# A fused attention and recurrence kernel: the last 128 queries turned token-major, batch statistics merged from three groups, and the recurrence's chunks started 10 steps ahead instead of 12

## The chip, the cores and the metric

The kernel runs on one core of one Trainium2 chip. The metric is the device time of one execution in microseconds. Each core has TensorE (PE, matrix products), VectorE (DVE), ScalarE (ACT), GpSimd (POOL) and SyncE (SP), which here only issues transfers. Each engine works through its own queue in order and waits for the others by semaphores; an instruction that waits holds up everything behind it on its engine.

## The reference, cut to what matters

```python
x = x + attention0(group_norm(x))            # 4 images, 128 channels, 64*64 pixels, full softmax
t = tokens(x)                                # (4, 4096, 128)
t = t + causal_attention(layer_norm(t))
l = layer_norm(t)
Wx = l @ W.T                                 # (4, 4096, 128)
mean, var = Wx.reshape(-1, 128).mean(0), Wx.reshape(-1, 128).var(0)   # over all 16384 tokens
Wx = (Wx - mean) * rsqrt(var + 1e-5) * gamma + beta
y = 0                                        # (4, 128)
for k in range(4096):
    y = sigmoid(Wx[:, k] + y @ V.T)          # V is orthogonal
    ys[:, k] = y
out = t + ys
```

Two things tie the end of the kernel together: the batch statistics need every token's `Wx`, that of the last token too, and the loop over 4096 tokens is serial in each of the four batches.

## The kernel before, in words

**Layout.** Data stand channel-major: 128 channels on the partitions, tokens along the free dimension. Attention goes batch by batch (`b`), layer by layer, in tiles of 512 queries (`c`), and inside a tile in units (`u`) of two key blocks of 128. `score(i)` makes the unit's scores on TensorE (`ps`) and their exponentials on ScalarE (`s`, with the causal mask of a diagonal block put on by GpSimd). `product(i)` adds `s` into the running `total` on VectorE and multiplies by the values on TensorE (`av`). The loop runs `score(i)`, a `step()` of side work, `product(i - 1)`. There are three buffers of `s`, so that an exponential waits for the add three units before it.

**The last tile.** The last 512 queries of the last batch are split into 384 and 128 (`LAST = 384`). The end of a tile is `finish` (divide by the sum of exponentials), `project` (W1v and the residual: `X2`), and `ffn` (deviation of each token, `FWc`, and the product of both into `WX`). For the last 128 queries before the change: the sums of exponentials are made for all 128 partitions by a product of `ones` with `total` (`pz`), inverted by a 128x128 reciprocal, multiplied with `av`, projected, transposed back to tokens for the deviation (`pt_f`), and the deviation is spread over the partitions by a product (`prow`). Then `bn_stats` goes over the last 512 columns, and `bn_aggr` over all 32 chunks' statistics (`fstats`), and from these come `fgain` and `fbias` of the batch normalization. `rsqrt` is one VectorE add and one GpSimd power.

**The recurrence.** Each batch's 4096 tokens are cut into chunks of 16, 16, 32 and 32 (`CHUNK`), and all chunks of a batch advance together. A chunk's start state is not known, so each starts from 0.5 and runs `WARM` steps on the tokens before its own; a sigmoid's slope is at most 1/4 and V keeps lengths, so that what is wrong at the start shrinks by four or more a step. At the end the states reached by the warm-up (`first`, `firstp`) are compared with the true ones (`ok`, bound `SAME = 2.0e-6`); if any differs by more, a general kernel is run after it. There are three chains side by side: batch 0, batch 1, and batches 2 and 3 together. One step of a chain is a product with V into PSUM (two passes, on top of the normalized input that VectorE has put there: `seed`) and one sigmoid on ScalarE (`move`, L1095). After `WARM` + 16 steps of all three, batches 2 and 3 go on alone for 16 more. `residual` adds the states to the kept activations and `store` sends them out.

`idle` issues products with zeros, whose results are not used. The tile framework orders the instructions of each engine and sets the semaphores; in a stretch under `manual_schedule` the order is that of the code.

## Time and profile before

| what | value |
|---|---|
| median of 3 runs | 2515.57 us (2515.12 to 2515.63) |
| profiled execution, its own time | 2515.47 us |
| its span, first to last instruction | 2513.7 us |
| mean granted TensorE clock | 0.997 |
| PE, DVE, ACT, POOL busy | 98%, 72%, 45%, 8% of the span |
| last product with values starts | 2432.45 us |
| first sigmoid of the recurrence starts | 2443.73 us |
| first sigmoid that writes a chunk's own token | 2459.20 us |
| batches 2 and 3 alone, from | about 2481 us |
| last residual ends, stores issued | 2498.96 us |

The profiled execution took 1.77 us more than its span, and lies 0.10 us under the median. In the profile's rows a line such as L995 is a line of the kernel's file; `out<-in` are the program's tile names without numbers; a fp32 product stands as two rows, one for each pass. The timeline view lists instructions in order of their start, merged where the same one repeats; its first two columns are start and duration in microseconds.

### The profile page before, as it was taken

What the parts mean: (1) busy time and instruction counts of PE and PEld (TensorE: products, weight loads), DVE (VectorE), ACT (ScalarE), POOL (GpSimd) and SP (SyncE); (2) the same over time, 40 slices, a digit from 0 to 9 for tenths busy, and PEclk for the clock granted to TensorE, in tenths of its full rate; (3) what the DMA queues carried; (4) which work ended last, traced back from release to release, by engine and by line L of the source; (5) the groups of instructions that cost most, each with busy time, mean ns of one, the idle gap of its engine ahead of it and who ended that gap; (6) DMA issues with size and microseconds to landing.
All of it is one profiled execution on the core that took longest, in us unless ns stands there. A gap on an engine that the chain in (4) does not pass through costs nothing.

```text
span 2513.7 us, 22498 instructions
## 1 busy us (share of the span) xinstructions
PE 2474.0 (98%) x7360; PEld 1342.9 (53%) x7360; DVE 1797.7 (72%) x3597; ACT 1121.9 (45%) x1399; POOL 210.8 (8%) x281
## 2 busy tenths in 40 slices
PE   7999999999999999999999999999999999999997
PEld 4555554444555555444455555444455555544465
DVE  6776669765877667866687676876677676786667
ACT  4444444444444444444444444444444444443456
POOL 2010002110000100210000010121000000010000
PEclk9999999999999999999999999999999999999998
DMA  2000001000100000100110000101010000010023
GB/s 75 9 17 9 17 9 42 21 22 13 46 17 9 17 9 22 36 24 13 35 33 14 12 13 13 34 25 26 13 46 17 9 17 9 17 26 17 9 76 136
DMA packets 154078, 64.40 MB, mean 26 GB/s; under 512 B 136160, under 2 KB 136928, under 8 KB 152160
## 3 DMA queue, kind: packets, MB, share of 16 engines
q1 hardware_dynamic: 151344, 59.27, 8.8%
q10 hardware_dynamic: 2608, 3.61, 0.4%
q8 instruction: 60, 0.98, 0.2%
q14 instruction: 66, 0.54, 0.1%
HBM read 31.66 MB, written 31.20 MB: 25 GB/s over the span
## 4 chain that ended last, share of the span: by engine, by line
PE 92%; DVE 4%; ACT 2%; issue 1%; POOL 1%; DMA 0%; SPq 0%; DVEq 0%; POOLq 0%
PE av L995 51%; PE ps L957 19%; PE ps L950 17%; PE pw_f L802 1%; PE pv L675 1%; PE pk L659 1%; PE pq L762 1%; PE po L858 1%; DVE total L992 1%; ACT WX L1095 1%; PE pz L1094 0%; ACT first L1095 0%; POOL X L656 0%; ACT WXp L1095 0%; DMA X<-in_x 0%
## 5 line engine op out<-in xcount | busy, mean ns | idle before, releaser
L992 DVE TENSOR_TENSOR total<-total,s 128x1024 f32<-128x1024 f32 (+5 forms) x810 | 882.9, 1094 | 537.7 <-ACT s L959 308.0
L995 PE MATMUL av<-s,WXp 128*128 128x512 f32 x2048 | 961.9, 592 | 0.0
L959 ACT ACTIVATE s<-ps,shift 128x1024 f32<-128x1024 f32 x512 | 569.9, 1114 | 759.5 <-PE ps L957 741.0
L957 PE MATMUL ps<-q,K 128*128 128x512 f32 x2048 | 757.9, 492 | 1.7 <-DVE K L670 1.6
L963 ACT ACTIVATE s<-ps,zero,R 128x512 f32<-128x512 f32 (+3 forms) x607 | 405.5, 718 | 510.6 <-PE ps L950 508.5
L995 PEld LDWEIGHTS av<-s,WXp 128*128 128x128 f32 x2048 | 384.2, 188 | 301.7 <-issue 259.9
L957 PEld LDWEIGHTS ps<-q,K 128*128 128x128 f32 x2048 | 386.0, 189 | 290.7 <-issue 232.3
L995 PE MATMUL av<-s,V 128*128 128x512 f32 (+3 forms) x1214 | 504.8, 538 | 1.3 <-POOL s L966 0.7
L950 PE MATMUL ps<-q,X 128*128 128x512 f32 (+3 forms) x1214 | 503.5, 537 | 0.0
L950 PEld LDWEIGHTS ps<-q,X 128*128 128x128 f32 x1214 | 224.9, 190 | 236.3 <-issue 219.5
L995 PEld LDWEIGHTS av<-s,V 128*128 128x128 f32 x1214 | 223.6, 190 | 230.5 <-issue 205.7
L571 POOL TENSOR_TENSOR rstd<-rstd,mhalf 128x4 f32<-128x4 f32 x32 | 32.4, 1012 | 1049.3 <-DVE rstd L570 1049.3
L966 POOL TENSOR_SCALAR_AFFINE_SELECT s<-s 128x128 f32<-128x128 f32 x128 | 52.5, 417 | 456.4 <-ACT s L963 455.8
L571 POOL TENSOR_TENSOR rstd_f<-rstd_f,mhalf 128x4 f32<-128x4 f32 (+2 forms) x33 | 47.4, 1436 | 507.9 <-DVE rstd_f L570 487.3
L656 POOL TENSOR_SCALAR X<-X,B0v 128x512 f32<-128x512 f32 x32 | 65.8, 2060 | 99.9 <-DVE xg L654 98.4
L754 DVE TENSOR_SCALAR V<-V,lmv,rstd 128x128 f32<-128x128 f32 x128 | 38.0, 342 | 33.6 <-POOL rstd L571 33.5
L689 DVE TENSOR_TENSOR q<-QR,qh 64x512 fp32r<-64x512 f32 x64 | 43.9, 686 | 6.7 <-PE ps L957 5.6
L671 ACT CAST K<-kh 64x512 fp32r<-64x512 f32 x32 | 19.7, 617 | 64.8 <-DVE kh L669 64.7
L826 DVE TENSOR_TENSOR t<-total 128x512 f32<-128x512 f32 x64 | 44.1, 689 | 4.4 <-PE pfw L615 2.5
L828 DVE STREAM_TRANSPOSE tt<-t 128x512 f32<-128x512 f32 x64 | 45.1, 705 | 1.6
L841 DVE STREAM_TRANSPOSE rb<-z 128x512 f32<-128x512 f32 x64 | 44.9, 702 | 1.0
L843 DVE SCALAR_TENSOR_TENSOR o<-rb,av 128x512 f32<-128x512 f32 x64 | 43.5, 680 | 2.7 <-DVE rb L841 0.5
(157 smaller groups left out, 1267.3 us busy)
## 6 DMA issues: line engine op xcount, KB each, us to landing
turn<-t SPq DMA_DIRECT2D x32, 256.0 KB, 2.0
V<-turn SPq DMA_DIRECT2D x128, 64.0 KB, 2.4
turn_f<-t_f SPq DMA_DIRECT2D x31, 256.0 KB, 2.0
t_f<-turn_f SPq DMA_DIRECT2D x124, 64.0 KB, 2.5
X<-in_x SPq DMA_DIRECT2D x28, 256.0 KB, 5.2
kept<-X SPq DMA_DIRECT2D x24, 256.0 KB, 2.0
Y<-kept SPq DMA_DIRECT2D x6, 1024.0 KB, 7.0
out<-Y SPq DMA_DIRECT2D x5, 1024.0 KB, 6.1
```

Of the source, the lines that this page charges most:

```text
L571: nc.gpsimd.tensor_tensor(dst, dst, mhalf[:, :n], ALU.pow)
L656: nc.gpsimd.tensor_scalar(xt, xt, B0v, None, ALU.add)
L826: nc.vector.tensor_tensor(t, total[:, 0, :w], total[:, 1, :w], ALU.add)
L828: nc.vector.transpose(tt, t)
L841: nc.vector.transpose(rb, z[:, :k].unsqueeze(2).to_broadcast([P, k, 32]))
L950: nc.tensor.matmul(ps[:, h, first[h] : w], lhsT=lhsT, rhs=q[:, off + first[h] : off + w], start=True, stop=True,)
L957: nc.tensor.matmul(ps[:, h, :], lhsT=lhsT, rhs=q[:, k, :], start=k == 0, stop=k == 1)
L959: nc.scalar.activation(s, ps, AF.Exp, bias=shift)
L963: nc.scalar.activation(part, ps[:, h, first[h] : w], AF.Exp, scale=scale, bias=zero)
L966: nc.gpsimd.affine_select(out=edge, in_=edge, pattern=[[1, P]], base=0, channel_multiplier=-1, compare_op=ALU.is_ge, fill=0.0,)
L992: nc.vector.tensor_tensor(t, t, s[:, h, f:w], ALU.add)
L995: nc.tensor.matmul(av[:, first[h] : w], lhsT=V[:, 2 * u + h, :], rhs=s[:, h, first[h] : w], start=u == 0 and h == 0, stop=2 * u + h == n - 1,)
```

## The change

The change touches only what surrounds the last 128 queries and the start of the recurrence.

1. `WARM` is 10 instead of 12.
2. The first step of every chunk needs no product: the state before it is 0.5 everywhere, so that V times it is a constant, added to beta once (`Fb0`, made in `merge1`). `first_step` is one ScalarE sigmoid from `WX` with the gain as scale. For all chunks but the last three of batch 3 it uses a gain and bias from the statistics without the last 128 queries (`scales["guess"]`); for those three it waits for the final ones.
3. The statistics have three groups in one tile `groups`: all full chunks but the last (`most_stats`, one `bn_aggr`), the 384 queries, and the 128 queries. `scale(9, ...)` gives the guess and `scale(15, ...)` the final gain.
4. The last 128 queries end in `last_part`, in an order written by hand. The sum of exponentials is a column with one token a partition (`pz_last`, products with one column of `ones`), the projection is made twice, once with tokens on the partitions (for the deviation) and once with channels (for `X2`), and the old activations are transposed ahead (`last_tokens`).
5. The states live in one tile `states` (768 columns, in the place of `QR`), cleared by GpSimd early. `pz_last` takes the last unit's exponentials directly, so the last add into `total` is gone.

```diff
-WARM = 12
+WARM = 10
...
+    def first_step(b, at, n, scales):
+        gain, bias = scales
+        l = CHUNK[b] - WARM
+        src = WX[b][:, l // 2, ds(at, n), l % 2]
+        nc.scalar.activation(first[b][:, ds(at + 1, n)], src, AF.Sigmoid, scale=gain, bias=bias)
...
+            nc.vector.bn_stats(groups[:, 3:9], WX[b][:, :, ds(c * QT // CHUNK[b], LAST // CHUNK[b]), :])
+            yield
+            whole(("most",))
+            gain, less = scale(9, "guess")
+            scales["guess"] = gain, shifted(gain, less, Fb0, "guess")
...
+        def scale(n, name):
+            mv = small.tile([P, 2], F32, name=f"mv_{name}")
+            nc.vector.bn_aggr(mv, groups[:, :n])
+            gain = const.tile([P, 1], F32, name=f"gain_{name}")
+            rsqrt(gain, mv[:, 1:2], 1e-5, 1)
+            less = const.tile([P, 1], F32, name=f"less_{name}")
+            nc.vector.tensor_scalar(less, mv[:, 0:1], -1.0, None, ALU.mult)
+            nc.vector.tensor_tensor(gain, gain, Fgamma, ALU.mult)
+            return gain, less
+
+        def most_stats():
...
+            nc.vector.bn_aggr(mv, stats_f.rearrange("p c s -> p (c s)"))
+            nc.vector.tensor_copy(groups[:, 1:2], mv[:, 0:1])
+            nc.vector.tensor_scalar(groups[:, 2:3], mv[:, 1:2], float(B * N - QT), None, ALU.mult)
...
+        def last_tokens():
+            pt = misc("pt_last")
+            nc.tensor.transpose(pt[:, :P], X[B - 1][:, ds(N - P, P)], ident)
+            scales["tok"] = tok = small.tile([P, C], F32, name="tok_last")
+            nc.scalar.copy(tok, pt[:, :P])
...
+        def last_part(av, pz, s):
...
+            avs = tmp.tile([P, QT], F32, tag="a", name="avs")[:, :w]
+            nc.vector.tensor_copy(avs, av[:, :w])
+            nc.scalar.activation(small.tile([P, 1], F32, name="sig"), s[:, 1, w - 1 : w], AF.Sigmoid)
+            for b in range(2):
+                first_step(b, 0, NC[b] - 1, scales["guess"])
+            rz = small.tile([P, 1], F32, name="rz")
+            nc.vector.reciprocal(rz, pz[:, 0:1])
+            ptok = wide[0][:, 0, :w]
+            nc.tensor.matmul(ptok, lhsT=avs, rhs=W1v, start=True, stop=True)
+            prz = wide[1][:, 0, :w]
+            nc.tensor.matmul(prz, lhsT=rz.to_broadcast([P, P]), rhs=ident, start=True, stop=True)
+            po = misc("po_last")[:, :w]
+            nc.tensor.matmul(po, lhsT=W1v, rhs=avs, start=True, stop=True)
+            idle(misc("idle_last"), 3)
+            tok = scales["tok"]
+            nc.vector.scalar_tensor_tensor(tok, ptok, rz, tok, ALU.mult, ALU.add)
+            rzs = tmp.tile([P, QT], F32, tag="b", name="rzs")[:, :w]
+            nc.scalar.copy(rzs, prz)
+            for b in range(2, B):
+                first_step(b, 0, NC[b] - 1 - (BEHIND if b == B - 1 else 0), scales["guess"])
...
+            nc.vector.bn_stats(stats, tok)
+            nc.vector.bn_aggr(mv, stats)
+            rsqrt(rstd, mv[:, 1:2], 1e-5, 1)
+            nc.vector.scalar_tensor_tensor(rzs, rzs, GUARD, po, ALU.mult, ALU.mult)
+            nc.vector.scalar_tensor_tensor(x2, rzs, 1.0 / GUARD, xt, ALU.mult, ALU.add)
+            nc.tensor.matmul(pw, lhsT=FWc, rhs=x2, start=True, stop=True)
+            prow = wide[0][:, 1, :w]
+            nc.tensor.matmul(prow, lhsT=rstd.to_broadcast([P, P]), rhs=ident, start=True, stop=True)
+            idle(misc("idle_last2"), 2)
+            nc.scalar.copy(raw, pw)
...
+            nc.vector.bn_stats(groups[:, 9:15], part)
+            scales["all"] = scale(15, "all")
...
-            if w == QT - LAST:
-                pz = misc(f"pz_{name}")
-                for h in range(2):
-                    nc.tensor.matmul(pz[:, :w], lhsT=ones, rhs=total[:, h, :w], start=h == 0, stop=h == 1)
-                idle(misc(f"idle_{name}"), 4)
-                rb = tmp.tile([P, QT], F32, tag="a", name=f"rb_{name}")[:, :w]
-                nc.vector.reciprocal(rb, pz[:, :w])
...
+            if last:
+                pz = misc("pz_last")
+                for h in range(2):
+                    nc.tensor.matmul(pz[:, 0:1], lhsT=total[:, h, :w], rhs=ones[:, 0:1], start=h == 0, stop=False)
...
+            if last:
+                for h in range(2):
+                    nc.tensor.matmul(pz[:, 0:1], lhsT=s[:, h, :w], rhs=ones[:, 0:1], start=False, stop=h == 1)
+                return av, pz, s
...
+        seed(0, 0)
+        bias = shifted(gain, less, Fbeta, "all")
+        seed(1, 0)
+        seed(2, 0)
+        bias0 = shifted(gain, less, Fb0, "all0")
+        first_step(B - 1, NC[-1] - 1 - BEHIND, BEHIND, (gain, bias0))
+        ordered.close()
...
-        for n in range(len(steps[2])):
+        for n in range(1, len(steps[2])):
```

The order of the built program on each engine differs from before only from the last tile on, but for three small things earlier: one product for `Fb0`, its add, and the clearing of `states` on GpSimd. On GpSimd, whose order around the last unit is short enough to tell, the queue before is: the last mask, the clears of `first`, the clear of `ok` (L1164), the power of `rstd_f`, the power of `fgain`. After the change it is: the power of `gain_guess`, the clear of `ok`, the last mask, the power of `rstd_last`, the power of `gain_all`.

## The prediction

> **What bounds the kernel now.** I read the page first (TensorE 98% busy, so the 2400 us of attention are untouched), then the chain of waits over the last 110 us, then the timeline of the handoff from the last product to the first sigmoid of the recurrence, then the windows view for the clock. All of what the change does lies after 2412 us.

> The chain of waits, in order of time (start, duration, what):

> ```profile
> 2431.21 0.87 issue
> 2432.45 0.50 PE av L995 x2
> 2433.01 0.57 POOL first L1067 x2
> 2433.69 0.93 DVE rb L820
> 2435.09 0.47 PE po L858 x2
> 2436.65 1.89 PE prow_f L566 x7
> 2439.20 0.70 DVE fstats L806
> 2439.92 1.03 DVE fmv L1051
> 2441.21 0.56 POOL fgain L571
> 2442.16 0.66 DVE py L1079
> ...
> 2449.79 0.86 ACT first L1095 x2
> 2451.08 0.86 ACT first L1095 x2
> ```

> The reader is to see a chain of single small instructions, from the last product at 2432.45 to 2443.73, where the first sigmoid starts: 11.28 us in which no engine is a bound. After it comes a beat: a step of the three chains each 1.29 us (2451.08 less 2449.79). The beat is the path itself, 12 + 16 times.

> The timeline of ScalarE:

> ```profile
> 2443.73 0.47 ACT L1095 ACTIVATE first<-py,fbias 128x255 f32<-128x255 f32 x1 [6.95 <-PE py L1094]
> ...
> 2459.20 0.50 ACT L1095 ACTIVATE WX<-py,fbias 128x256 f32<-128x256 f32 x1
> ```

> and of GpSimd around the last mask:

> ```profile
> 2432.11 0.29 POOL L966 TENSOR_SCALAR_AFFINE_SELECT s<-s 128x128 f32<-128x128 f32 x1 [4.30 <-ACT s L963]
> ...
> 2433.76 0.74 POOL L1164 MEMSET ok<- 128x768 f32 x1
> 2437.15 0.55 POOL L571 TENSOR_TENSOR rstd_f<-rstd_f,mhalf 128x1 f32<-128x1 f32 x1 [2.65 <-DVE rstd_f L570]
> ```

> The warm-up took 2459.20 - 2443.73 = 15.47 us, exactly 12 x 1.289: no step is lost. Before, GpSimd made the mask at once (0.07 us after its exponential) and cleared `ok` later, in nobody's way.

> **The change part by part.** I follow the built program's queues with the rows' durations, and with the trace's own hand-over times (0.05 us ScalarE or VectorE to TensorE, 0.04 TensorE to VectorE or ScalarE, 0.08 VectorE to GpSimd, 0.035 from a VectorE result to the next VectorE instruction).

> *Added ahead of the last unit.* `most_stats` puts a bn_aggr of 186 numbers (the 192 of `fmv` took 1.02) and two 128x1 operations (0.16 each) into VectorE's queue at 2414.5. VectorE is full from 2414.8 to 2421.7; it had 0.28 us idle there, so it comes out about 0.8 to 1.0 late. Behind it stands the add of unit 802, which frees the buffer for the exponential of unit 805 (three buffers): it ended at 2419.54 for a start at 2420.05, 0.4 of slack after the hand-over. So the attention's end is 0.4 late (0 if the slack elsewhere takes it, 0.6 at most). The transposed tokens (one pass 0.11 on TensorE, a copy of 0.27 on ScalarE) fall into the same gap and add nothing. `Fb0` costs TensorE one 128x1 product, under 0.1. The clearing of `states` (0.74 by the row of `ok`, the same size) waits for reads long done and stands before a power for layer 1 that is needed a tile later: nothing; were that cover gone, 0.7 once.

> *The guess, and what queues behind it.* VectorE now does, between the adds of units 812 to 814: bn_stats of 384 columns (rows: 0.30 for 128, 0.69 for 512, so 0.56), bn_aggr 0.18, an add 0.15, a negation 0.15. The add for the guess ends near 2432.7, and then GpSimd's queue holds in order the power (0.55), the clear of `ok` (0.74) and only then the last mask (0.29). So the mask ends at 2432.8 + 1.58 = 2434.35 instead of 2432.40: **1.95 late**, 0.4 of it from above. TensorE's second half of the last product waits for it, and behind that everything. On TensorE itself the column sums of `total` stand before the last unit's products and wait for the add of unit 814, which ends near 2433.3: an idle of 2 us, hidden behind the mask. I take the two GpSimd rows as they are; at the low end (a clear of nothing) the mask would be limited by that add, 0.6 earlier.

> *From the mask to the first sigmoid.* Before: 2432.40 to 2443.73, 11.33 us. Now, in order: last product 0.05 + 0.49; copy of `av` 0.04 + 0.29 (the 128x128 copies from PSUM in `merge1` took 0.29); token-major projection, from the end of its operand 0.61 (as o to po before: 2434.94 to 2435.55), 2435.75; the fused multiply-add 0.04 + 0.29; bn_stats 0.035 + 0.30; bn_aggr 0.035 + 0.18; add 0.035 + 0.15, which is 2436.8. From here the two branches part. The deviation's power on GpSimd (0.08 + 0.55) is done at 2437.45. VectorE meanwhile makes X2 by two operations of 0.29, also 2437.45, and the product with FWc (0.05 + 0.49) and its copy by ScalarE (0.04 + 0.27) end at 2438.3; the spread deviation's product lies beside this copy. Then 128x128 product 0.29, bn_stats of 128 columns 0.30 (before: 512, 0.69), bn_aggr of 15 numbers 0.18 (before: 1.02), add 0.15, power 0.55, times gamma 0.16, with hand-overs 2440.2. First seed: 255 columns instead of 510; no row has that size, so it lies between 0.29 (128 columns) and 0.745 (510), and by the slope of about 1.05 ns a column of the 128 to 512 rows it is 0.48; then the product 0.05 + 0.69. First sigmoid at **2441.6, 2.1 us earlier** than 2443.73. The 128x128 reciprocal (0.96), four 128x128 passes of `pz`, the transposition and 1.2 us of bn_stats and bn_aggr left the path; the late mask ate most of it. The early sigmoids of step 1 (0.47 each for 255 columns) run in ScalarE's idle 6.95 us; the copies behind them there are ready first.

> *Fewer steps.* The first sigmoid is now that of the second of 10 steps, so 9 steps stand between it and the first own token instead of 12. 3 x 1.289 = 3.87. Against it a rough start: the three late columns of batch 3 hold back the pair's product (ScalarE 0.13 to 0.2, TensorE 0.6), and VectorE still owes the second seeds (0.745 each, three in a row) when the first sigmoids ask for them. Following the queues the 9 steps take 12.13 instead of 11.60: 0.53 lost. **Gain 15.47 - 12.13 = 3.34.**

> *After it.* Order and counts of the last 16 + 16 steps, residuals and stores are the same, shifted. The kept activations load behind the last product (row of SP at 2433.01, landing by about 2447); 2 us later they land by 2449, and VectorE first wants them near 2459. Nothing.

> Sum: 2.13 + 3.34 = 5.47, rounded 5.5. The profiled execution took 2515.47, so 2510.0; it lies 0.1 under the median of the runs, which I neglect.

> [...] For TensorE's clock the windows view says (length, busy time of PE, PEld, DVE, ACT, POOL, then granted clock, DMA):

> ```profile
> 2431.20:2434.60 3.40, 2.59 (x12) 1.72 (x12) 2.30 (x7) 2.29 (x4) 1.79 (x5) 1.00 0.24 46
> 2434.60:2438.00 3.40, 2.36 (x11) 1.79 (x12) 1.24 (x7) 0.27 (x1) 0.55 (x1) 1.00 0.95 369
> ...
> 2443.70:2459.20 15.50, 15.50 (x71) 11.70 (x72) 14.24 (x21) 15.14 (x36) 0.00 (x0) 1.00 0.06 26
> ...
> 2500.00:2508.00 8.00, 0.59 (x2) 0.50 (x2) 2.96 (x7) 0.00 (x0) 0.00 (x0) 0.55 1.00 413
> ```

> A mean clock of 0.55 over 8 us means full speed for 0.8 us and half after: the clock fell near 2500.8, some 3.1 us after the recurrence's last product. [...]

> **The rivals.** *The late mask costs less.* If GpSimd's clear overlaps or the guess is earlier, the add of unit 814 limits: 0.6 more gain, and another 0.2 to 0.4 if the aggregate ahead is hidden. 2509.0 to 2509.4. For it: GpSimd's spans are rough. Against it: the queue order is fixed.

> *More is lost at the start.* VectorE's three seeds of 0.745 in a row pace the first steps, and the added aggregate costs 0.6 or more: gain 4 to 5, 2510.6 to 2511.6, within what counts as no change. For it: VectorE was busy 14.24 of 15.50 in the warm-up. Against it: before, the same six seeds cost no step.

> *The clock falls in the handoff* (slower). Each step at half clock costs 1.29 more; the gain is used up after 4.3 such steps (5.5 us), from there on the kernel is slower: with 8 slow steps, 2510.0 + 10.3 = about 2520. [...]

> *It does not do what it says.* Ten steps must bring the states within 2e-6. Worked out in double precision from the reference's inputs, what is left is 1.6e-7 after 10 and 4e-6 after 8: the general kernel stays unused. I give it under 1%.

> **How the numbers follow.** 0.2% of 2515.57 is 5.03 us, about what a measurement of this kernel can tell from no change; the line is 2510.54. Forecast: chance 0.64, with the unknown durations 2509.2 to 2510.9; 0.58 of it beyond the line. Smaller cost of the mask: 0.20, all beyond. More lost at the start: 0.12, within. Clock or fallback: 0.04, slower. Faster 0.78, same 0.18, slower 0.04. The range, 2508.6 to 2511.8, takes in the first three cases with their bounds and leaves out the fourth and the ends.

> **What would show it.** Right: the last mask ends about 2 us after its exponential, behind a power and a clear on GpSimd; bn_stats of 128 columns and a bn_aggr of about 0.18 on the path; the first `states` sigmoid from PSUM about 2 us earlier than 2443.73; about 12.1 us from it to the first `WX` sigmoid; clock 1.00 throughout. Wrong: a mask at once (then 2509.3); steps of more than 1.29, or a clock under 1 in 2434 to 2445; VectorE waiting for the loads of Y; the last product more than 0.6 late before the mask.

## The result, and the profile after

The changed kernel took 2510.56 us in the median of 17 runs (2509.59 to 2512.05), the kernel before 2515.28 (17 runs, 2514.52 to 2515.82): 4.72 us less, a ratio of 0.9982 with a 95% interval of 0.9976 to 0.9989. The forecast was 2510.0 and 5.5 us. The profiled execution of the changed kernel took 2510.21 us, span 2508.5.

Two profiled executions do not start alike: the exponential of unit 800, before anything of the end is touched, starts at 2415.49 before and at 2414.86 after. So stretches are compared, not clock times: from the end of the last exponential to the first sigmoid that writes a chunk's own token it was 27.16 us before (2432.04 to 2459.20) and is 22.20 after (2431.53 to 2453.73). The first row of the table below is therefore not the change's: the profiled execution of the changed kernel was already 1.09 us ahead at 80 us.

The chain of waits of the changed kernel, in order of time (start, duration, what):

```profile
2431.79 0.72 POOL gain_guess L579
2432.51 0.69 POOL ok L1276
2433.20 0.26 POOL s L1068
2433.46 0.04 issue
2433.50 0.50 PE av L1103 x2
...
2434.37 0.79 PE last L878 x2
...
2436.02 1.29 PE idle_last L574 x3
2437.31 0.04 issue
2437.35 0.50 PE pw_last L900 x2
...
2438.50 0.31 DVE groups L911
2438.83 0.23 DVE mv_all L837
```

The reader sees that the 128x128 reciprocal (`rb`, 0.93) is gone from the chain, and that the two statistics steps of 0.70 and 1.03 us are now `groups` 0.31 and `mv_all` 0.23. New at the head of the chain stand three GpSimd steps in a row, power, clear, mask, as the queue order said. And something nobody wants is on it: 1.29 us of products with zeros.

The timeline of ScalarE after (the last column tells the idle time before the row, and what ended it):

```profile
2441.49 0.47 ACT L1198 ACTIVATE states<-py,bias_all 128x255 f32<-128x255 f32 x1 [3.34 <-PE py L1197]
2441.86 0.38 ACT L594 ACTIVATE states<-WXp,bias_all,gain_all 128x3 f32<-128x3 f32 x1
...
2443.02 1.34 ACT L1198 ACTIVATE states<-py,bias_all 128x254 f32<-128x254 f32 x3 [0.42 <-PE py L1197]
2444.71 9.06 ACT L1198 ACTIVATE states<-py,bias_all 128x255 f32<-128x255 f32 x21 [0.35 <-PE py L1197]
2453.73 0.50 ACT L1198 ACTIVATE WX<-py,bias_all 128x256 f32<-128x256 f32 x1
```

Nine steps took 12.24 us (2453.73 less 2441.49), 0.64 more than 9 x 1.289; two waits of ScalarE, 0.42 and 0.35, carry the loss. The windows view of the handoff (length, busy time of PE, PEld, DVE, ACT, POOL, then granted clock, DMA share, GB/s):

```profile
2430.45:2433.87 3.42, 1.66 (x14) 1.38 (x13) 2.00 (x9) 2.48 (x5) 1.66 (x3) 1.00 0.00 0
2433.87:2437.28 3.41, 3.25 (x13) 2.36 (x11) 1.88 (x8) 1.88 (x5) 0.56 (x1) 0.50 0.64 183
2437.28:2440.69 3.41, 2.81 (x13) 1.79 (x12) 1.71 (x9) 0.27 (x1) 0.54 (x1) 1.00 1.02 425
```

The clock fell to half for one window of 3.413 us, which the prediction had as a rival, with the wrong size. (In this trace the clock is 1.00 from 17.229 to 2433.866 us, half to 2437.279, 1.00 to 2495.305: 708 times, once and 17 times 3.413 us; in the trace of before it is 1.00 from 22.794 to 2500.871, 726 times. A window here is one piece of such a grid.) That is why the zero products stand on the chain: three of them took 1.63 us and `pw_last` started at 2437.35, though its operand was ready at 2436.91.

| stretch of the profiled execution, us | before | after | difference |
|---|---|---|---|
| start to the exponential of unit 800 | 2415.49 | 2414.86 | -0.62 |
| to the end of the last exponential | 16.55 | 16.67 | +0.12 |
| to the end of the last mask | 0.37 | 1.92 | +1.55 |
| to the first sigmoid from PSUM | 11.33 | 8.04 | -3.29 |
| to the first own token | 15.47 | 12.24 | -3.22 |
| to the end of the span | 54.54 | 54.74 | +0.21 |

### The profile page after: what moved, and what is told of

The parts are those of the page before. It is cut to its first block, busy times and chain, and to the rows that moved or that the text cites. A ratio compares the mean times of both kernels' runs of the same rounds, so it can differ in the third digit from the quotient of the medians.

```text
span 2508.5 us, 22447 instructions
## 1 busy us (share of the span) xinstructions
PE 2467.6 (98%) x7341; PEld 1338.6 (53%) x7341; DVE 1794.4 (72%) x3604; ACT 1120.8 (45%) x1397; POOL 211.8 (8%) x281
## 4 chain that ended last, share of the span: by engine, by line
PE 92%; DVE 4%; ACT 2%; issue 1%; POOL 1%; DVEq 0%; POOLq 0%; ACTq 0%
PE av L1103 51%; PE ps L1059 19%; PE ps L1052 17%; PE pw_f L819 1%; PE pv L702 1%; PE pq L789 1%; DVE total L1100 1%; PE po L951 1%; PE pk L686 1%; ACT WX L1198 1%; ACT states L1198 0%; PE pz L1197 0%; ACT WXp L1198 0%; POOL X L683 0%; ACT s L1061 0%
## 5 line engine op out<-in xcount | busy, mean ns | idle before, releaser
L579 POOL TENSOR_TENSOR rstd_f<-rstd_f,mhalf 128x4 f32<-128x4 f32 (+1 forms) x32 | 46.8, 1464 | 505.6 <-DVE rstd_f L578 485.0
```

The lines of the kernel that those rows point to most:

```text
L579: nc.gpsimd.tensor_tensor(dst, dst, mhalf[:, :n], ALU.pow)
```

## The experiments

The order is that of the question: first the parts of the change by themselves, then its two costs (the queue in front of the mask, the clock), then what beats it. A few tenths between two variants lie inside the intervals of both; there the traces carry the reading, and the medians only agree with it or not.

**Ten steps alone.** The kernel before, with `WARM` and the indices that hang on it:

```diff
-WARM = 12
+WARM = 10
...
-            if WARM < n < last and (n + 1) % 4 == 0:
+            if WARM < n < last and (n - WARM) % 4 == 3:
```

> The kernel before with WARM = 10 (and the indices of seeds and residuals that follow from it), nothing else: first step with a product, one set of statistics, the old end of the last tile. The term 'fewer steps' of the prediction says two steps of 1.289 us: 2.58 below the kernel before, and 10 steps from the first sigmoid to the first own token taking 12.9 us. If VectorE's seeds paced the warm-up (a rival of the prediction), it would be less, 1.5 to 2.2. The other 2.1 of the 4.7 that the change gained would then belong to the handoff and the skipped first step.

2512.63 us in the median of 13 runs beside 2515.15 of the kernel before: 2.52 less, ratio 0.999 (0.9982 to 0.9999). In its trace the first own token comes 12.89 us after the first sigmoid, ten steps of 1.289. The step of 1.289 was the right measure, and VectorE's seeds did not pace the warm-up. More than half of the 4.7 us is a constant.

**The first step undone.** The changed kernel with ten real steps:

```diff
-                    nc.gpsimd.memset(states, 0.0)
+                    nc.gpsimd.memset(states, 0.5)
...
-            for b in range(2):
-                first_step(b, 0, NC[b] - 1, scales["guess"])
...
-            t = int(k == 0)
+            t = 0
...
-        for n in range(1, len(steps[2])):
+        for n in range(len(steps[2])):
```

(The first column of each batch is still cleared, and all calls of `first_step` are gone.)

> The changed kernel with its first step undone: states set to 0.5, all ten steps with a product, first seeds over both steps (510 columns instead of 255), no sigmoids on the guess; the rest (three groups, last_part, WARM = 10) stays. By the prediction's sum the skipped step was worth 1.29 less a rough start of 0.53, and the shorter first seed another 0.27: 1.0 more than the changed kernel, 3.7 below the kernel before; ten steps take 12.9. If the rough start comes from the first seeds and not from the late columns, it would stay here: 13.4 to 13.5 for ten steps, and 1.5 more than the changed kernel.

2511.56 us (21 runs; before 2515.29): 3.73 less than before, ratio 0.9986 (0.9980 to 0.9993). That is 1.0 more than the changed kernel, as the sum of the prediction has it (1.29 - 0.53 + 0.27). Ten steps took 12.86 us in its trace, so there is no rough start here: it comes with the skipped first step and its late columns, not with the length of the first seeds. By the medians the change is 2.5 us of two steps, 1.0 of the skipped one, and 1.2 of the new end of the last tile.

**The clear behind the mask.** The clear of `ok` on GpSimd is made to read the final bias, which puts it last:

```diff
-        nc.gpsimd.memset(ok, 0.0)
+        nc.gpsimd.tensor_scalar(ok.rearrange("p (k s) -> p k s", s=NC[2])[:, :, 0], bias.to_broadcast([P, 6]), 0.0, None, ALU.mult)
```

> The changed kernel, but the clear of ok (0.73 us on GpSimd, ahead of the last mask) is replaced by a clear of six columns that reads the final bias and so stands at the end of GpSimd's queue. Queue theory as the prediction had it (the mask alone releases the last product): mask 0.73 earlier, 0.7 less time than the changed kernel, about 5.4 below the kernel before. Rival: TensorE's own queue is right behind it (column sums of total, first half, column sum end at 2433.2 in the changed kernel's profile, the mask at 2433.46): only 0.3 less, about 5.0 below before. Clock theory: the thin window of TensorE stays thin, so the granted clock still falls to half for 3.4 us between 2430 and 2440.

2509.97 us (21 runs; before 2515.15): 5.18 less than before, ratio 0.9980 (0.9973 to 0.9986), 0.46 better than the change. The timeline of TensorE in this kernel says why it is not 0.7:

```profile
2432.01 0.61 PE L1088 MATMUL pz_last<-ones,total 128*128 128x1 f32 x4 [1.47 <-DVE total L1100]
2432.47 0.47 PE L1103 MATMUL av<-s,V 128*128 128x128 f32 x2
2432.78 0.28 PE L1111 MATMUL pz_last<-ones,s 128*128 128x1 f32 x2
2432.92 0.47 PE L1103 MATMUL av<-s,V 128*128 128x128 f32 x2
```

The mask ended at 2432.61 (1.24 us behind its exponential instead of 1.92), but TensorE's own queue reached the masked half only at 2432.92. The delay of the start fell from 1.97 to 1.55 us, 0.42: two queues stood in front of one instruction. The prediction had the second only in its rival, where the add of unit 814 was to limit 0.6 earlier. The clock fell in this trace too, at 2433.89.

**Fillers in the gap.** Five products with zeros where TensorE idled 1.48 us:

```diff
-                pz = misc("pz_last")
+                pz = misc("pz_last"); idle(misc("fill"), 5)
```

> The changed kernel with five products with zeros (128x512, 0.235 us each by the rows at full clock) on TensorE ahead of the column sums of total, where it was idle for 1.48 us. Clock theory: the 3.41 us ahead of the handoff are then about 80% busy instead of 48%, the granted clock stays 1.00 through 2430 to 2446, ptok's product takes 0.5 instead of 0.79, the three fillers 0.7 instead of 1.63, pw_last starts when X2 is ready: 0.8 less from mask to first sigmoid (7.25 instead of 8.03), about 5.5 below the kernel before, and the runs lie as close together as those of the kernel before (1.3 us from lowest to highest, the changed kernel 2.5). Rival one: the slow products are beside waits of VectorE and nothing is gained (4.7 below before). Rival two: the fillers stand in the way of the column sums: slower by up to 0.3.

The same three windows in the profile of this kernel:

```profile
2430.45:2433.87 3.42, 2.67 (x16) 1.95 (x16) 2.02 (x9) 2.47 (x5) 1.66 (x3) 1.00 0.00 0
2433.87:2437.28 3.41, 2.67 (x20) 2.15 (x18) 1.96 (x8) 1.91 (x6) 0.56 (x1) 1.00 0.62 187
2437.28:2440.69 3.41, 2.89 (x13) 1.64 (x11) 2.33 (x10) 0.25 (x1) 0.54 (x1) 1.00 1.01 423
```

The clock stays at 1.00, and its timeline shows what that is worth:

```profile
2434.39 0.49 PE L878 MATMUL last<-W1v,avs 128*128 128x128 f32 x2
...
2435.14 0.93 PE L574 MATMUL idle_last<-nil 128*128 128x512 f32 x3
2436.77 0.46 PE L900 MATMUL pw_last<-X,FWc 128*128 128x128 f32 x2 [0.70 <-DVE X L898]
```

`last` 0.49 instead of 0.79, `idle_last` 0.93 instead of 1.63, `pw_last` waits for its operand again, and the first sigmoid stands 7.40 us behind the mask instead of 8.04. But the median was 2510.34 us (16 runs, 2509.25 to 2511.54; before 2515.15): 4.81 less than before, ratio 0.9980 (0.9973 to 0.9988), only 0.1 better than the change, and the runs lie nearly as wide apart. So the expected 0.8 and the narrow spread were wrong: the dip costs 0.64 us in an execution that has it, and not every execution of the changed kernel does. The profiles of `behind_guess` and `first_product`, whose products up to `pw_last` are those of the changed kernel, show no dip and 7.41 and 7.68 us (the second with 0.27 for its longer first seed); those of the changed kernel, of `ok_late` and of the repeat below show it. What differs between them is where the window lies (table below). The spread of this kernel is left open.

**No fillers at all.**

```diff
-            idle(misc("idle_last"), 3)
...
-            idle(misc("idle_last2"), 2)
...
-                idle(ps.rearrange("p t h s -> p (t h s)"), 1)
```

> The changed kernel without its eleven products with zeros (three idle_last, two idle_last2, six on py); nothing that is computed is left out. Clock theory (the granted clock follows the busy share of the window before, and some 50% is too little): the windows from 2433.9 on hold about half and then a fifth of a window of products, so the clock stays at half from the first thin window into the first steps of the recurrence, 7 to 11 us in all; 2 to 4 steps at up to 1.29 us more each and the small products at twice their time: 2 to 5 us above the changed kernel, 2512.5 to 2515.5, and the slow steps are seen as sigmoids of states more than 0.5 us apart. [...]

10761.57 us (6 runs), and the clock theory is not judged by that number: the comparison at the end found states too far apart, and the general kernel ran behind the fast one. The expectation's words that nothing computed is left out were wrong. The six products on `py` are no fillers. In the code they are the products with `start=True` on these tiles; VectorE's seeds and the steps' products, which have no `start=True`, come after. That they matter is shown by the next run, which leaves out only the other five and stays on the fast kernel (2511.10 us); what of them the steps need, no run isolates. What the stretch ahead of the verdict shows is still of use: the clock was at half from 2435.12 for three windows, and back at 2445.36; the first sigmoid came 8.31 us after the mask and the nine steps took 13.19. Together 1.85 us more than in `fill`, for 10.24 us of half clock, some of it inside the steps.

**Without the five true fillers.** The `py` products stay:

```diff
-            idle(misc("idle_last"), 3)
...
-            idle(misc("idle_last2"), 2)
```

> The changed kernel without its five products with zeros idle_last (3) and idle_last2 (2); the six on py stay. Clock theory by streamed columns (windows of 0.15 to 0.22 closed the gate, 0.43 and more did not): the two windows behind the mask come down from 0.43 to 0.68 to about 0.25 to 0.5, so that the clock falls in more of the runs and stays down longer: median 0.3 to 0.8 above the changed kernel. [...]

2511.10 us (21 runs; before 2515.06): 3.96 less than before, ratio 0.9984 (0.9978 to 0.9991), 0.7 more than the unaltered changed kernel beside it. All 21 executions have a mean granted clock of 0.996; of the changed kernel's it was 3 of 17 and 4 of 18. In its profile two windows run at half:

```profile
2432.20:2435.61 3.41, 2.53 (x18) 2.17 (x18) 1.42 (x7) 2.33 (x6) 1.22 (x3) 1.00 0.20 43
2435.61:2439.03 3.42, 1.95 (x6) 1.56 (x7) 1.79 (x9) 0.80 (x3) 0.55 (x1) 0.50 0.96 371
2439.03:2442.44 3.41, 3.41 (x10) 2.53 (x8) 2.71 (x9) 0.27 (x1) 0.54 (x1) 0.50 1.00 416
2442.44:2445.85 3.41, 3.06 (x14) 2.12 (x12) 2.93 (x5) 2.63 (x8) 0.00 (x0) 1.00 0.93 389
```

The first of them is 2.53 of 3.41 us busy, its longest idle stretch 0.33 us, and yet the clock falls behind it. So the busy column does not tell such windows from the others (1.94 of 3.41 us in `first_product` left the clock full). The row of a 128-column pass lasts 0.28 us, while the next one starts 0.11 us behind it. Counted by this spacing of starts in the traces, as the time in which columns stream (0.11 us for a pass of 128 columns, 0.235 for a product with zeros, nothing for one column), the windows that began at full clock sort themselves without exception:

| window (kernel) | streamed share of it | clock of the next |
|---|---|---|
| 2430.40 (repeat), 2430.45 (changed) | 0.13, 0.15 | half |
| 2430.48 (`ok_late`) | 0.16 | half |
| 2431.71 (`no_fill`) | 0.27 | half |
| 2432.20 (`no_fill2`) | 0.32 | half |
| 2491.50 (`first_product`, the last steps) | 0.38 | full |
| 2430.06 (`first_product`) | 0.39 | full |
| 2429.23 (`behind_guess`) | 0.40 | full |
| 2432.50 (`best`) | 0.46 | full |
| 2430.41 (`fill`) | 0.50 | full |
| 2432.60 (before) | 0.53 | full |

The counts that the expectation names, 0.22 and 0.43, come out as 0.27 and 0.39 in this one. Neither the busy column nor the longest idle stretch sorts them: 1.95 us busy with an idle of 1.47 left the clock full in `behind_guess`, 2.53 us busy with 0.33 halved it here. At half clock the passes of 128 columns start 0.21 us apart instead of 0.11 (changed kernel, 2434.74 to 2435.60). Counted at 0.11 all the same, the half-clock windows of the handoff had 0.17 to 0.21 where the next was half again (`no_fill`, `no_fill2`) and 0.41 to 0.53 where the next was full (0.41 in the changed kernel). That is what these windows show; shares between 0.32 and 0.38 were not seen.

None of the windows of the table was without products, neither the changed kernel's (1.66 us busy) nor that of `no_fill2` (2.53), and leaving out five products with zeros cost 0.7 us.

**The three late chunks on the guess.** Their first step stands ahead of the first sigmoid from PSUM:

```diff
+            first_step(B - 1, NC[-1] - 1 - BEHIND, BEHIND, scales["guess"])
             nc.vector.bn_stats(groups[:, 9:15], part)
...
-        bias0 = shifted(gain, less, Fb0, "all0")
-        first_step(B - 1, NC[-1] - 1 - BEHIND, BEHIND, (gain, bias0))
```

> The changed kernel, but the first step of the three late chunks of batch 3 uses the guess of gain and bias as all others do, and stands right behind the copy of pw_last, before the first sigmoid from PSUM; the second bias (0.21 us on VectorE between the seeds) is gone. The warm-up took 12.24 us for nine steps, 0.64 more than 9 x 1.289. If the three late columns cost that (ScalarE 0.38, and the pair's product waits for them), about 0.4 goes: 11.8 to 11.9 from the first sigmoid to the first own token, 5.1 below the kernel before. If VectorE's second seeds (0.70 each, three in a row) pace the start, as the prediction's other half has it: 0.2 at most, from the bias that is gone.

2510.28 us (14 runs; before 2515.29): 5.01 less than before, ratio 0.9981 (0.9973 to 0.9989), 0.3 better than the change. ScalarE's timeline:

```profile
2438.01 0.39 ACT L594 ACTIVATE states<-WXp,bias_guess,gain_guess 128x3 f32<-128x3 f32 x1 [0.35 <-DVE WXp L907]
2441.00 1.38 ACT L1198 ACTIVATE states<-py,bias_all 128x255 f32<-128x255 f32 x3 [2.60 <-PE py L1197]
2442.56 0.47 ACT L1198 ACTIVATE states<-py,bias_all 128x255 f32<-128x255 f32 x1 [0.18 <-PE py L1197]
2443.21 9.67 ACT L1198 ACTIVATE states<-py,bias_all 128x255 f32<-128x255 f32 x22 [0.18 <-PE py L1197]
2452.84 0.50 ACT L1198 ACTIVATE WX<-py,bias_all 128x256 f32<-128x256 f32 x1
```

Nine steps in 11.85 us instead of 12.24; the waits are now 0.18 and 0.18. The late columns were 0.40 of the 0.64; the cause of the other 0.24 is not isolated.

**Both costs together**, `early_h0`: the clear last, and on TensorE the unmasked half of the last product ahead of the column sums of `total`, behind two fillers. **And with the late chunks**, `best`.

```diff
+                idle(misc("fill"), 2)
+                for h in range(2):
+                    nc.tensor.matmul(av[:, :w], lhsT=V[:, 2 * u + h, :], rhs=s[:, h, :w], start=False, stop=h == 1)
+                    nc.tensor.matmul(pz[:, 0:1], lhsT=s[:, h, :w], rhs=ones[:, 0:1], start=h == 0, stop=h == 1)
+                    for k in range(2 - 2 * h):
+                        nc.tensor.matmul(pz[:, 0:1], lhsT=total[:, k, :w], rhs=ones[:, 0:1], start=False, stop=False)
```

> The changed kernel with three edits together: the clear of ok at the end of GpSimd's queue; on TensorE the first half of the last product and its column sum ahead of the column sums of total (it needs no mask and no total, so it fills the wait for total); and two products with zeros ahead of it. If queue and clock are the two costs, each goes: the second half starts at about 2432.85 instead of 2433.50 (0.65) and the clock stays at 1.00 (0.8): 1.4 less than the changed kernel, about 6.1 below the kernel before, or 2509.2. If only the queue counts: 0.65 less, 5.4 below. If VectorE or ScalarE (table load to 2432.8) release the next step: no gain from the queue, 5.5 below or less.

> early_h0 (clear of ok last, first half of the last product ahead of the column sums, two products with zeros) and the late three chunks on the guess together. If the parts add: early_h0's 5.7 below the kernel before plus 0.4 = 6.1, about 2509.05, and 11.8 from first sigmoid to first own token. If VectorE's seeds pace the start: 5.7 to 5.9.

`early_h0` took 2509.46 us (12 runs; before 2515.15), 5.69 less than before, ratio 0.9977 (0.9969 to 0.9986), `best` 2509.31 (12 runs; before 2515.29), 5.98 less, ratio 0.9976 (0.9968 to 0.9985). Expected were 6.1 for each. In both traces the last half starts 0.05 behind the mask, the clock stays at 1.00, and the first sigmoid stands 7.40 us behind the mask. The parts add: 0.97 for queue and clock, 0.3 for the late chunks. The runs of both lie within 1.4 us.

**The mask first.** In `best` the mask still waits for the guess's power. Here the variance of the guess takes 0 times a masked value, so that GpSimd must do the mask first; both halves stand ahead of the sums of `total`, and the early sigmoids behind the two copies of ScalarE.

```diff
+                nc.vector.scalar_tensor_tensor(gain, s[:, 1, P - 1 : P], 0.0, gain, ALU.mult, ALU.add)
+                nc.gpsimd.tensor_tensor(gain, gain, mhalf[:, :1], ALU.pow)
```

> The kernel best, with the last mask ahead of the guess's power on GpSimd too (the guess's variance takes 0 times a masked value, so it waits for the mask), both halves of the last product ahead of the column sums of total, and the early sigmoids behind the copies of rzs and raw_last on ScalarE. Queue theory: the mask ends 0.36 after its exponential as in the kernel before, instead of 1.24; the last half starts 0.85 earlier, so 0.8 less than best: 6.8 below the kernel before, about 2508.5. Rival: the guess is now behind the mask and comes late: the column for rz waits for the sums of total, VectorE's products with gamma stand ahead of the token-major sum, and a part of it, 0.3 to 0.5, is given back.

2509.01 us (10 runs; before 2515.06): 6.05 less than before, ratio 0.9976 (0.9967 to 0.9986). GpSimd and VectorE in its timeline:

```profile
2432.10 0.29 POOL L1075 TENSOR_SCALAR_AFFINE_SELECT s<-s 128x128 f32<-128x128 f32 x1 [4.29 <-DVE mv_guess L835]
2432.83 0.55 POOL L842 TENSOR_TENSOR gain_guess<-gain_guess,mhalf 128x1 f32<-128x1 f32 x1 [0.43 <-DVE less_guess L844]
```

```profile
2433.54 0.17 DVE L879 RECIPROCAL rz<-pz_last 128x1 f32<-128x1 f32 x1 [0.27 <-PE pz_last L1099]
2433.63 0.14 DVE L880 TENSOR_TENSOR gain_guess<-gain_guess,Fgamma 128x1 f32<-128x1 f32 x1
2433.80 0.22 DVE L586 SCALAR_TENSOR_TENSOR bias_guess<-less_guess,gain_guess,Fb 128x1 f32<-128x1 f32 x1
```

The mask ends 0.37 behind its exponential, as before the change, 0.87 us earlier than in `best`; 0.36 are given back between mask and first sigmoid (7.77 instead of 7.41), through `rz` and the guess's two products in VectorE's queue. So the rival holds beside the queue theory: the first own token stands 19.99 us behind the last exponential instead of 20.49. Of this 0.50 the medians show 0.07, which is inside what they can tell apart; in its one profile the stretch from the first own token to the end is 1.05 us longer than in `best` (55.75 instead of 54.70), where a single wait of SyncE near the end took 1.07. It is the lowest median of the study, though not shown to be below `best`.

**The changed kernel again**, as the base of the last three.

> The changed kernel, unaltered, on the same chip as the two below, as their base and as a second profile. Clock theory: whether its clock falls depends on where the free-running windows of 3.413 us lie; in the profiles of kernels with the same handoff it fell where a window began at 2430.45 (mask to first sigmoid 8.04 us) and did not where it began at 2429.2 or 2430.06 (7.41). So it is either 8.0 with a dip or 7.4 without, nothing between; 4.7 below the kernel before, and 12.24 to the first own token in both cases.

2510.37 us (18 runs; before 2515.06): 4.69 less, ratio 0.9982 (0.9975 to 0.9989). Its profile has the window from 2430.40, the dip, 8.05 us from mask to first sigmoid, and 12.24 to the first own token: the same to 0.01 us in each stretch of the handoff. The windows do not begin with the span: their edges at 17.229 us (changed) and 22.794 us (before) lie 2.15 us apart on a grid of 3.413.

## Why the prediction was right, and where it was not

The forecast, a gain of about 5.5 us with the median inside 2509.2 to 2510.9, held; the measured gain is 4.7. Point by point:

- *Fewer steps, 3.34.* Measured 3.22 in the profile (15.47 less 12.24). The rough start was 0.64 instead of 0.53. Two steps alone gave 2.52, the skipped one 1.0. Right, and for the reason given: of the 0.64, 0.40 are the three late columns (`behind_guess`).
- *From the mask to the first sigmoid, 7.25.* 7.41 in the executions without a dip, 8.04 with one. The working was 0.16 short there. (Its sum slips by 0.08 at the token-major projection, 2435.22 + 0.61, and takes the same back in the last step.)
- *The mask, 1.95 late.* 1.67 late: 1.55 between exponential and mask, and 0.12 of the attention's end, where 0.4 was put for the aggregate of `most_stats` on VectorE; its slack took most of that. The step "TensorE's second half of the last product waits for it, and behind that everything" held: that half started 0.05 behind the mask. Its next limit, TensorE's own queue, was named with the add of unit 814 and put 0.6 earlier; in `ok_late` it took over after 0.42 of the 0.73 us of the clear.
- *The clock.* The prediction gave a fall of the clock 0.04, as a part of "Clock or fallback", and asked for 1.00 throughout. That it would stay there with 11 products with zeros in place of 22 was the author's estimate, which no run shows: the clock fell in the profile, though TensorE's longest idle ahead of it was 1.48 us and not the 2 us that the prediction put behind the mask. What the traces show in its place are windows of 3.413 us: with 0.13 to 0.32 of one streamed the next was half, with 0.38 to 0.53 full. The rival's price was wrong as well. It set 1.29 us for a step at half clock and up to 10 us in all; measured were 0.64 us for one window, 3.25 of 3.41 us busy with the small products and three products with zeros, and the clock was back at 1.00 at 2437.28, 4.21 us before the first sigmoid. Where steps did run at half clock, in `no_fill` for 3.43 us, they lost 0.95 (13.19 instead of 12.24).
- *After it, nothing.* From the first own token to the end of the last residual it is 39.73 to 39.77 us in every trace that keeps to the fast kernel. But the end of the span moves by itself: from the first branch past the verdict to the end it is 8.74 us in the profile of before, 8.91 with ten steps alone, 8.91 to 9.40 in the nine profiles of the changed form, and 9.94 in `mask_first`.

So the handoff without a dip gained 5.47 at the first own token (27.16 - 21.57, less the 0.12), the sum of the prediction. That it fits so closely is luck: the attention's end came 0.28 less late than put, and the stretch behind the mask and the steps took 0.16 and 0.11 more.

The 0.8 that the median lacks lies outside of it, and some 0.43 of it comes with the change. Set against the kernel before, exponential by exponential, all eleven profiles of the changed form fall back by 0.22 or 0.23 us between 83 and 89 us and by 0.20 to 0.23 between 1594 and 1604; `warm10_only` does at neither place. The first is where the product for `Fb0` stands on TensorE. The same stretch of its stream, after and before:

```profile
82.67 1.45 PE L1103 MATMUL av<-s,WXp 128*128 128x512 f32 x3
83.95 0.28 PE L642 MATMUL pfw<-half,FV 128*128 128x1 f32 x2
84.09 1.17 PE L1059 MATMUL ps<-q,K 128*128 128x512 f32 x4
85.11 1.45 PE L1103 MATMUL av<-s,WXp 128*128 128x512 f32 x3
```

```profile
83.76 1.45 PE L995 MATMUL av<-s,WXp 128*128 128x512 f32 x3
84.65 1.49 PE L957 MATMUL ps<-q,K 128*128 128x512 f32 x4
85.97 1.45 PE L995 MATMUL av<-s,WXp 128*128 128x512 f32 x3
```

From the first row to the last it is 2.44 us instead of 2.21. The prediction put `Fb0` at "under 0.1". At the second place VectorE's last add of a tile starts 0.12 behind the end of the one before it instead of overlapping it (0.34 after that one's start before, 0.54 after it now); why it does so is open. The rest of the 0.8 is 0.64 in those executions that have a dip, and 0.2 to 0.5 in the stretch behind the verdict. That the latter belongs to the change, and not to where code lies or how an execution falls, is not shown; with one profile of the kernel before it stays open.

## What to carry to other kernels

Ahead of an instruction that several queues release, work out the second queue as well: taking 0.73 us off the first gave 0.42. The change that shortened the serial work on TensorE's path also thinned its stream, from 0.53 streamed in the thinnest window of the handoff to 0.15, and the clock was half for the next 3.413 us. Count columns, not busy rows (2.53 of 3.41 us busy stood ahead of half clock in `no_fill2`), over such a stretch, and cover the gap with work that can run early (half of a product behind two fillers gave 0.46 and a clock of 1.00 in `best`) before reaching for fillers alone. A product of one column, put into a stream that TensorE bounds, cost 0.22 us here: price it by the stream, not by its size. And before calling a product with zeros a filler, try the kernel without it: leaving out five cost 0.7 us here, leaving out the six on `py` too brought in the general kernel (10761.57 us).
